# A selective-scan stage on one core: an earlier copy of dt * x to PSUM, B and C fetched apart, and empty pieces ahead of statistics

## The chip, the cores and the metric

The kernel runs as one program on one core of a Trainium2 chip. The metric is the device time of one execution in microseconds. The time before is the median of 3 runs.

## What is computed

The reference passes eight images of 56 x 56 positions and 128 channels through four layers. Layers 0, 2 and 3 are deformable convolutions with a small network behind them. Layer 1, which the change touches, is a "SS2D" block: a layer norm, a projection to 256 channels and a gate, a depthwise 3 x 3 convolution, a selective scan in four directions over all 3,136 positions, and an output part.

```python
x_dbl = jnp.einsum('bkdl,kcd->bkcl', xs, x_proj_w)
dts, Bsm, Csm = jnp.split(x_dbl, [R, R + N], axis=2)
dt = jax.nn.softplus(einsum('bkrl,kdr->bkdl', dts, dt_projs_w) + dt_projs_b)
A = -jnp.exp(A_logs).reshape(K, Di, N)
def step(h, t):
    dt_t, u_t, B_t, C_t = t
    h = h * jnp.exp(dt_t[..., None] * A) + (dt_t * u_t)[..., None] * B_t[:, :, None, :]
    y = jnp.einsum('bkdn,bkn->bkd', h, C_t)
    return (h, y)
...
y = _ln(y, out_norm_w, out_norm_b) * silu(z)
x = x + einsum('bhwd,cd->bhwc', y, out_proj_w)
x = x + fc2(gelu(fc1(_ln(x, norm2_w, norm2_b))))
```

There are Di = 256 channels with N = 16 states each, and K = 4 directions.

## The kernel before

**Tiling of the scan.** The positions of an image are cut into 4 chunks of SC = 784. A step is one image, one direction and one chunk: 8 x 4 x 4 = 128 steps, the directions in the order 1, 3, 0, 2. A step has 32 units. A unit holds 32 channels x 4 states on the 128 partitions and 784 positions along the free dimension. Units are numbered t = 4 cg + sg: cg is one of 8 groups of channels, sg one of 4 groups of states. "Group" below means the four units of one cg, "unit 4n" the first unit of group n.

**A unit.** `decay` (L1299) makes dA = exp(dt * A) on ACT into PSUM (two buffers). `inputs` (L1305, L1309) makes u = dt * x * B: for sg 0, 1 and 2 on VectorE (L1309), reading dt * x from PSUM, and for sg 3 on GpSimd (L1305, tile `up`), reading it from SBUF. The scan itself is one VectorE instruction (L1400, tile h, three buffers); its last column is kept for the next chunk by ACT (L1403). GpSimd multiplies with C (L1405, tile hc, six buffers). PE adds the 4 states of a channel (`add_sums`, L1331) into the PSUM tile `acc`, which `open_sums` (L1323) starts and `close_sums` (L1342, ACT) copies out every eight units.

**The copy.** `spread` (L1293) brings dt * x of one group into the PSUM tile `dtu`, which has one buffer, by two multiplications with the identity on PE. The new copy has to wait for the u of unit sg = 2 of the group before, the last that VectorE makes from that tile. It is asked for at the start of the iteration with sg = 2, two units ahead of its use.

**Fetches.** B and C of a step lie in DRAM in the tensor `rows`. `fetch_rows` (L1238) brings both for four states in one DMA, each row repeated over 32 partitions, into the tile bc (128 x 2 x 784, 784 KB, NSG + 1 = 5 buffers). The four fetches for the next step are asked for at t = 25, 29, 30, 31. `fetch_dt` (L1245) brings dt and dt * x of a group, two groups ahead, three buffers. All DMAs are issued from SP's queue.

**Work beside the scan.** `prepare` makes dt, B and C of the next step; it is a generator that is resumed at every even t. `input_stage` (the next image's norm, projection and convolution) and `output_stage` (norm, gate, projection, the two-layer network; 8 calls per image) are generators cut into pieces by `yield`; `advance(1)` runs one piece. It is called at odd t and where t % 8 == 4, which makes 20 places in a step, and at every t in the direction 2 of the last image. A piece is a few matmuls into the single-buffered PSUM tile `misc` and what reads them: `output_stage` transposes y on PE (L1130), takes statistics on VectorE (L1026, L1027), and later adds the projection to x on VectorE (L1153). Pieces left over at the end run after the last scan.

**What sets the order.** The program is traced in the order of the Python code, and a scheduler then sets the order of each engine's queue, which the engine keeps; `issue_after` (in `add_sums`) keeps the sums behind the last copy traced. The program order is therefore a wish and not the order of the queue.

Of the kernel before, what the change touches and what calls it, by code (L numbers as in the profile page):

```python
# [41 lines left out]
F32 = mybir.dt.float32  # L42
# [73 lines left out]
SC, SR = 784, 14  # L116
# [13 lines left out]
TC, TS = 32, 4  # L130
NCG, NSG = DI // TC, NST // TS
# [815 lines left out]
class Vss:  # L947
# [168 lines left out]
    def output_stage(self, i, c):  # L1116
        nc, w, n, T, m = self.nc, self.w, SH // self.NT, self.NT, SH
        y = self.bg.tile([128, NCH, m], F32, name="yin", tag="yin")
        nc.sync.dma_start(out=y, in_=self.sums[i][:, :, m * c : m * (c + 1)])
        sg = self.bg.tile([128, NCH, m], F32, name="sg", tag="sg")  # L1120
        nc.sync.dma_start(out=sg, in_=self.gates[i][:, NCH:, m * c : m * (c + 1)])
        yield
        yield
        z = self.bg.tile([128, T, DI], F32, name="z", tag="z")
        for t0 in range(0, T, 2):
            ps = self.misc()
            for t in range(2):
                at = n * (t0 + t)
                for ch in range(NCH):
                    nc.tensor.transpose(ps[:n, DI * t + 128 * ch : DI * t + 128 * (ch + 1)], y[:, ch, at : at + n], self.net.ident)  # L1130
            yield
            srcs = [ps[:n, DI * t : DI * (t + 1)] for t in range(2)]
            rs = self.stats(srcs)
            yield
            self.normalize(z[:, t0 : t0 + 2], srcs, rs)
            yield
        xt = self.bg.tile([128, T, C], F32, name="xt", tag="xt", bufs=2)
        nc.sync.dma_start(out=xt[:n], in_=self.rows_of(self.src[i], c, n))
        gT = self.bg.tile([128, NCH, m], F32, name="gT", tag="gT")
        for ch in range(NCH):  # L1140
            ps = self.misc()
            self.transpose(ps, [z[:n, t, 128 * ch : 128 * (ch + 1)] for t in range(T)])
            nc.scalar.activation(gT[:, ch, :], ps[:, :m], AF.Identity, bias=w["now_b"][:, ch : ch + 1], scale=w["now_w"][:, ch : ch + 1])
            yield
        nc.gpsimd.tensor_mul(gT, gT, sg)
        yield
        yield
        po = self.misc()
        for t in range(T):
            for ch in range(NCH):  # L1150
                nc.tensor.matmul(po[:n, 128 * t : 128 * (t + 1)], lhsT=gT[:, ch, n * t : n * (t + 1)], rhs=w["out"][:, ch, :], start=ch == 0, stop=ch == NCH - 1)
        yield
        nc.vector.tensor_add(xt[:n], xt[:n], po[:n].rearrange("p (t c) -> p t c", c=128))  # L1153
        srcs = [xt[:n, t, :] for t in range(T)]
        rs = self.stats(srcs)
        yield
        z = self.bg.tile([128, T, C], F32, name="z", tag="z", padded_shape=[128, T, DI])
        self.normalize(z, srcs, rs)
        yield
        ps = self.misc()  # L1160
        self.transpose(ps, [z[:n, t, :] for t in range(T)])
        xT = self.bg.tile([128, m], F32, name="xT", tag="xT")
        nc.scalar.activation(xT, ps[:, :m], AF.Identity, bias=w["n2b"], scale=w["n2w"])
        yield
        pre = self.bg.tile([128, NF, m], F32, name="pre", tag="pre", padded_shape=[128, NF, LC])
        for f in range(NF):
            ps = self.misc()
            nc.tensor.matmul(ps[:, :m], lhsT=w["fc1"][:, 128 * f : 128 * (f + 1)], rhs=xT, start=True, stop=True)
            nc.scalar.activation(pre[:, f, :], ps[:, :m], AF.Identity, bias=w["fc1_b"][:, f : f + 1])
            yield  # L1170
        last = nc.scalar.activation(pre, pre, AF.Gelu_apprx_tanh)
        with self.tc.issue_after(last.ins):
            nc.scalar.preload_act_table_set(EXP_LN)
        yield
        po = self.misc()
        self.net.bias_row(po, n, w["fc2_b"], T)
        for t in range(T):
            for f in range(NF):
                nc.tensor.matmul(po[:n, 128 * t : 128 * (t + 1)], lhsT=pre[:, f, n * t : n * (t + 1)], rhs=w["fc2"][:, f, :], start=False, stop=t == T - 1 and f == NF - 1)
            if t % 2:  # L1180
                yield
        nc.vector.tensor_add(xt[:n], xt[:n], po[:n].rearrange("p (t c) -> p t c", c=128))
        yield
        nc.sync.dma_start(out=self.rows_of(self.dst[i], c, n), in_=xt[:n])
        yield
# [44 lines left out]
            nc.sync.dma_start(out=s["dd"][128 * h : 128 * (h + 1)], in_=dd.rearrange("p x e -> p (x e)"))  # L1230
            yield

    def fetch_rows(self, s, sg):

        t = s["bc", sg] = self.work.tile([128, 2, SC], F32, name="bc", tag="bc", bufs=NSG + 1)
        r = s["rows"]
        src = bass.AP(tensor=r.tensor, offset=r.offset + TS * sg * 2 * SC, ap=[[0, TC], [2 * SC, TS], [1, 2 * SC]])
        self.nc.sync.dma_start(out=t.rearrange("p x e -> p (x e)"), in_=src)  # L1238

    def fetch_dt(self, s, cg):  # L1240

# [12 lines left out]
    def scans(self):  # L1254
        nc, w = self.nc, self.w
# [6 lines left out]
        units = [(at, t) for at in range(len(steps)) for t in range(NT)]  # L1262
# [5 lines left out]
            pass  # L1268
        for x in range(2):
            self.fetch_dt(state[0], x)  # L1270
        for x in range(NSG):
            self.fetch_rows(state[0], x)
        tasks = deque()

        def advance(count):
# [8 lines left out]
        def on_pool(t):  # L1284

            return order[t][1] == NSG - 1

        def spread(at, t):

            s, (cg, sg) = state[at], order[t]  # L1290
            ps = s["dtu", cg] = self.pdtu.tile([128, 2, 512], F32, name="dtu", tag="dtu")
            for b in range(2):
                last = nc.tensor.matmul(ps[:, b, :SH], lhsT=self.net.ident, rhs=s["dt", cg][:, 1, SH * b : SH * (b + 1)], start=True, stop=True)  # L1293
            self.last_spread = last.ins

        def decay(at, t):
            (i, k, c), s, (cg, sg) = steps[at], state[at], order[t]
            da = s["dA", t] = self.pda.tile([128, 1024], F32, name="dA", tag="dA")
            nc.scalar.activation(da[:, :SC], s["dt", cg][:, 0], AF.Exp, scale=w["A"][:, k, NSG * cg + sg : NSG * cg + sg + 1])  # L1299

        def inputs(at, t):
            s, (cg, sg) = state[at], order[t]
            if on_pool(t):
                u = self.work.tile([128, SC], F32, name="up", tag="up", bufs=1)
                nc.gpsimd.tensor_mul(u, s["dt", cg][:, 1], s["bc", sg][:, 0])  # L1305
            else:
                u = self.work.tile([128, SC], F32, name="u", tag="u", bufs=2)
                halves = [v.rearrange("p (x e) -> p x e", x=2) for v in (u, s["bc", sg][:, 0])]
                nc.vector.tensor_mul(halves[0], s["dtu", cg][:, :, :SH], halves[1])  # L1309
            s["u", t] = u  # L1310

# [43 lines left out]
        st = ready = None  # L1355
        group, late = [], deque()
        zeros = self.zeros()
        for x, (at, t) in enumerate(units):
            (i, k, c), s, (cg, sg) = steps[at], state[at], order[t]
            forward = k < 2  # L1360
            if t == 0:
# [8 lines left out]
                        self.load_xb(i + 1)  # L1370
                    ready = self.prepare(state[at + 1], *steps[at + 1][1:])
            if t % (2 * NSG) == 0:
                late.append((x + 5, open_sums, (at, t)))
            if sg == NSG - 2 and x + 2 < len(units):
                spread(*units[x + 2])
            while late and late[0][0] <= x:
                _, do, args = late.popleft()
                do(*args)
            if t % 2 == 0:
# [5 lines left out]
                    self.fetch_dt(state[to[0]], to[1])  # L1385
            if t in (3, 19):
                next(zeros, None)
            for g, when in enumerate((25, 29, 30, 31)):
                if t == when and at + 1 < len(steps):
                    self.fetch_rows(state[at + 1], g)  # L1390
            if x + 1 < len(units):
                decay(*units[x + 1])
                if not on_pool(units[x + 1][1]):
                    inputs(*units[x + 1])
            if x + 2 < len(units) and on_pool(units[x + 2][1]):
                inputs(*units[x + 2])
            hh = self.work.tile([128, SC], F32, name="h", tag="h", bufs=3)
            step = 1 if forward else -1
            u, dA = s.pop(("u", t)), s.pop(("dA", t))
# [2 lines left out]
                last = SC - 1 if forward else 0  # L1402
                nc.scalar.copy(st[:, t : t + 1], hh[:, last : last + 1])  # L1403
            hc = self.work.tile([128, SC], F32, name="hc", tag="hc", bufs=6)
            nc.gpsimd.tensor_mul(hc, hh, s["bc", sg][:, 1])  # L1405
            group.append((order[t], hc))
            if t % 2:
                late.append((x + 3, add_sums, (at, group)))
                group = []
                if t % (2 * NSG) == 2 * NSG - 1:  # L1410
                    late.append((x + 5, close_sums, (at, t)))
            if t % 2 or t % 8 == 4 or (i == self.images - 1 and k == 2):
                advance(1)
        for _ in zeros:
            pass
# [79 lines left out]
```

## Time and profile before

| | us |
|---|---|
| median of 3 runs (18,864.26 to 18,886.17) | 18,885.19 |
| the profiled execution, its own time | 18,880.74 |
| its span, first to last instruction | 18,879.1 |
| mean granted clock of PE | 0.802 |
| first unit of the scan to the last product | 2,450 to 14,006 |
| scan, L1400, from u (3,072) and from up (1,024), mean | 1.838 and 1.836 |
| u, L1309 (3,072), mean | 0.957 |
| hc, L1405 (4,096), mean | 1.871 |
| up, L1305 (1,024), mean | 1.854 |
| dA, L1299 (4,096), mean | 0.914 |

The profile is of one execution. Its first part gives each engine's busy time over the whole span, which holds three other layers. A row of windows gives, for a stretch of time, its length, the busy time and the count of records of PE, the weight load, DVE (VectorE), ACT (ScalarE) and POOL (GpSimd), then the granted clock of PE, the share of DMA and GB/s. A row of waits names who waited, for whom, and then us in total, times, and the longest. A row of the timeline has start, length, engine, line, operation, tiles and count, and in brackets the idle time ahead of it with what ended it. An fp32 matmul leaves two records.

### The profile page before, as it was taken

How to read it: one execution, taken by the hardware profiler on the slowest of the kernel's cores; microseconds unless marked ns; L12 is line 12 of the kernel's file. 1: busy time of each engine (PE TensorE's matmuls, PEld its weight loads, DVE VectorE, ACT ScalarE, POOL GpSimd, SP SyncE). 2: the span in 40 equal slices, each digit the busy share in tenths (PEclk: the TensorE clock that was granted, in tenths of full speed). 3: DMA queues.
4: the chain of work that ended last, by engine and by line, in shares of the span. 5: the costliest groups of instructions: out<-in, count | busy, mean ns of one | idle time of the engine just before them, and what ended most of it. 6: DMA issues, size and time to landing. Idle time of an engine off the chain costs nothing. (4 is left out here: it accounts for less than half of the span.)

```text
span 18879.1 us, 237115 instructions
## 1 busy us (share of the span) xinstructions
PE 14376.3 (76%) x79747; PEld 6872.9 (36%) x79747; DVE 15314.2 (81%) x18794; ACT 11192.3 (59%) x21363; POOL 11749.8 (62%) x6462
## 2 busy tenths in 40 slices
PE   6888777678778778778778778777666888577777
PEld 4555422222222222222222222222224666455555
DVE  7777379988988988988888889888967777677776
ACT  4665555566656666566566656656554666455555
POOL 1121079989988989989989989988961122111111
PEclk6777788889888888888888888888876777676666
DMA  8887544444433433444343443343326888588777
GB/s 240 227 222 217 133 156 158 164 156 155 146 138 142 142 141 142 143 144 142 140 143 138 145 143 140 141 146 131 141 99 172 216 214 211 155 205 211 206 211 178
DMA packets 1250535, 3112.19 MB, mean 165 GB/s; under 512 B 76608, under 2 KB 868180, under 8 KB 1181468
## 3 DMA queue, kind: packets, MB, share of 16 engines
q1 hardware_dynamic: 1249292, 3096.75, 53.5%
q8 instruction: 641, 10.50, 0.2%
q14 instruction: 602, 4.93, 0.1%
HBM read 2400.54 MB, written 872.17 MB: 173 GB/s over the span
## 5 line engine op out<-in xcount | busy, mean ns | idle before, releaser
L1405 POOL TENSOR_TENSOR hc<-h,bc 128x784 f32<-128x784 f32 x4096 | 7565.3, 1871 | 1008.9 <-DVE h L1400 774.5
L1400 DVE TENSOR_TENSOR_SCAN h<-dA,st,u 128x784 f32<-128x784 f32 x3072 | 5578.6, 1838 | 384.2 <-ACT dA L1299 267.4
L1299 ACT ACTIVATE dA<-dt,v_A 128x784 f32<-128x784 f32 x4096 | 3741.0, 914 | 787.1 <-DVE h L1400 783.5
L1331 PE MATMUL acc<-hc,v_sum 128*32 128x392 f32 x16384 | 3391.2, 563 | 89.2 <-POOL hc L1405 88.9
L1309 DVE TENSOR_TENSOR u<-dtu,bc 128x784 f32<-128x784 f32 x3072 | 2885.5, 957 | 586.7 <-PE dtu L1293 461.0
L1293 PE MATMUL dtu<-dt,ident 128*128 128x392 f32 x4096 | 2097.8, 639 | 1341.3 <-issue 932.4
L769 PE MATMUL pt<-ident,sw 112*128 112x112 f32 (+8 forms) x11648 | 1907.1, 302 | 476.5 <-DMA sw<-skew 470.4
L736 POOL MEMSET win<- 128x1820 f32 (+2 forms) x384 | 631.6, 1648 | 2487.8 <-DMA skew<-win 1950.0
L1400 DVE TENSOR_TENSOR_SCAN h<-dA,st,up 128x784 f32<-128x784 f32 x1024 | 1879.6, 1836 | 262.2 <-POOL hc L1405 132.9
L771 ACT COPY st<-pt 128x448 f32<-128x448 f32 (+6 forms) x2912 | 1228.7, 443 | 1326.3 <-PE pt L769 1282.6
L1403 ACT COPY st<-h 128x1 f32<-128x1 f32 x3072 | 580.1, 189 | 2276.1 <-DVE h L1400 2267.2
L1305 POOL TENSOR_TENSOR up<-dt,bc 128x784 f32<-128x784 f32 x1024 | 1898.5, 1854 | 36.5 <-DVE h L1400 30.9
L733 POOL TENSOR_TENSOR ay<-hat,om 112x756 f32<-112x756 f32 (+2 forms) x192 | 442.6, 2305 | 2154.2 <-ACT hat L729 1882.0
L1331 PEld LDWEIGHTS acc<-hc,v_sum 128*32 128x32 f32 x16384 | 800.8, 119 | 2600.5 <-issue 1711.8
L1293 PEld LDWEIGHTS dtu<-dt,ident 128*128 128x128 f32 x4096 | 855.0, 232 | 2403.2 <-issue 1474.4
L769 PEld LDWEIGHTS pt<-ident,sw 112*128 112x128 f32 (+8 forms) x11648 | 1336.6, 171 | 1056.7 <-issue 691.9
L745 DVE TENSOR_TENSOR win<-win,patch 112x252 f32 (+2 forms) x3456 | 1561.0, 461 | 52.9 <-DVE bn_st L847 14.4
L742 DVE TENSOR_TENSOR patch<-ay,hat 112x756 f32<-112x756 f32 (+2 forms) x1152 | 1221.7, 1074 | 446.7 <-POOL ay L733 446.4
L780 PE MATMUL yps<-st,xw 120*32 120x48 f32 (+8 forms) x23296 | 1221.0, 295 | 234.6 <-ACT st L771 190.6
L1069 PE MATMUL misc<-xn,v_tap 128*128 128x448 f32 x2016 | 882.3, 583 | 117.6 <-ACT xn L1103 63.3
L822 PE MATMUL ps<-xT,w_fc 128*128 128x448 f32 (+1 forms) x1536 | 800.1, 655 | 112.5 <-ACT xT L817 72.2
L1342 ACT COPY y<-acc 64x392 f32<-64x392 f32 x768 | 576.2, 750 | 450.3 <-PE acc L1331 440.5
(163 smaller groups left out, 19374.7 us busy)
## 6 DMA issues: line engine op xcount, KB each, us to landing
dt<-dds SPq DMA_DIRECT2D x1024, 784.0 KB
bc<-rows SPq DMA_DIRECT2D x512, 784.0 KB
sw<-skew SPq DMA_DIRECT2D x224, 1050.0 KB
sw<-skew SPq DMA_DIRECT2D x224, 896.0 KB
dds<-dd SPq DMA_DIRECT2D x256, 784.0 KB
sw<-skew SPq DMA_DIRECT2D x224, 784.0 KB
skew<-win SPq DMA_DIRECT2D x128, 964.7 KB
skew<-win SPq DMA_DIRECT2D x128, 771.8 KB
```

Of the source, the lines that this page charges most:

```text
L742: nc.vector.tensor_mul(patch[:n], bcast(a, 3, KX), bcast(b, 2, KY))
L745: self.last_add = nc.vector.tensor_add(to, to, patch[:n, NCB * p : NCB * (p + 1)]).ins
L769: last = nc.tensor.transpose(ps[:KP, n * g : n * (g + 1)], sw[t0:t1, g, KP * j : KP * (j + 1)], self.net.ident[t0:t1, t0:t1])
L771: nc.scalar.copy(st[:KP, : G * n], ps[:KP, : G * n])
L780: self.nc.tensor.matmul(yps[CG * g : CG * (g + 1), t0:t1], lhsT=xw[:KP, j, CG * g : CG * (g + 1)], rhs=st[:KP, n * g : n * (g + 1)], start ...
L1293: last = nc.tensor.matmul(ps[:, b, :SH], lhsT=self.net.ident, rhs=s["dt", cg][:, 1, SH * b : SH * (b + 1)], start=True, stop=True)
L1299: nc.scalar.activation(da[:, :SC], s["dt", cg][:, 0], AF.Exp, scale=w["A"][:, k, NSG * cg + sg : NSG * cg + sg + 1])
L1305: nc.gpsimd.tensor_mul(u, s["dt", cg][:, 1], s["bc", sg][:, 0])
L1309: nc.vector.tensor_mul(halves[0], s["dtu", cg][:, :, :SH], halves[1])
L1331: nc.tensor.matmul(acc[r : r + TC, :SH], lhsT=w["sum"], rhs=hc[:, SH * b : SH * (b + 1)], start=False, stop=sg == NSG - 1)
L1400: nc.vector.tensor_tensor_scan(hh[:, ::step], dA[:, :SC][:, ::step], u[:, ::step], st[:, t : t + 1], ALU.mult, ALU.add)
L1405: nc.gpsimd.tensor_mul(hc, hh, s["bc", sg][:, 1])
```

## The change

`spread` is asked for one iteration earlier (sg = NSG - 3), for three units ahead, directly after the `inputs` of the last u that reads the old copy. B and C get a tile, a fetch and five buffers each; B is asked for at t = 25, 28, 29, 30, C at t = 26, 29, 30, 31. `output_stage` gets an empty piece between the transposes of y and their statistics (twice per call) and one between the output projection and the addition that reads it. `advance` is called at t % 4 == 0 where it was t % 8 == 4, so 24 times in a step. The loop's variable x is renamed now.

```diff
@@ output_stage
                     nc.tensor.transpose(ps[:n, DI * t + 128 * ch : DI * t + 128 * (ch + 1)], y[:, ch, at : at + n], self.net.ident)
             yield
+            yield
             srcs = [ps[:n, DI * t : DI * (t + 1)] for t in range(2)]
             rs = self.stats(srcs)
...
         yield
+        yield
         nc.vector.tensor_add(xt[:n], xt[:n], po[:n].rearrange("p (t c) -> p t c", c=128))
@@ fetches
-    def fetch_rows(self, s, sg):
-
-        t = s["bc", sg] = self.work.tile([128, 2, SC], F32, name="bc", tag="bc", bufs=NSG + 1)
+    def fetch_row(self, s, x, sg):
+
+        name = "bc"[x]
+        t = s[name, sg] = self.work.tile([128, SC], F32, name=name, tag=name, bufs=NSG + 1)
         r = s["rows"]
-        src = bass.AP(tensor=r.tensor, offset=r.offset + TS * sg * 2 * SC, ap=[[0, TC], [2 * SC, TS], [1, 2 * SC]])
-        self.nc.sync.dma_start(out=t.rearrange("p x e -> p (x e)"), in_=src)
+        src = bass.AP(tensor=r.tensor, offset=r.offset + TS * sg * 2 * SC + x * SC, ap=[[0, TC], [2 * SC, TS], [1, SC]])
+        self.nc.sync.dma_start(out=t, in_=src)
@@ scans
-        for x in range(NSG):
-            self.fetch_rows(state[0], x)
+        for g in range(NSG):
+            for x in range(2):
+                self.fetch_row(state[0], x, g)
...
-            if sg == NSG - 2 and x + 2 < len(units):
-                spread(*units[x + 2])
-            while late and late[0][0] <= x:
+            while late and late[0][0] <= now:
...
-            for g, when in enumerate((25, 29, 30, 31)):
-                if t == when and at + 1 < len(steps):
-                    self.fetch_rows(state[at + 1], g)
-            if x + 1 < len(units):
-                decay(*units[x + 1])
-                if not on_pool(units[x + 1][1]):
-                    inputs(*units[x + 1])
+            for x, when in enumerate(((25, 28, 29, 30), (26, 29, 30, 31))):
+                if t in when and at + 1 < len(steps):
+                    self.fetch_row(state[at + 1], x, when.index(t))
+            if now + 1 < len(units):
+                decay(*units[now + 1])
+                if not on_pool(units[now + 1][1]):
+                    inputs(*units[now + 1])
+                if sg == NSG - 3 and now + 3 < len(units):
+                    spread(*units[now + 3])
...
-            if t % 2 or t % 8 == 4 or (i == self.images - 1 and k == 2):
+            if t % 2 or t % 4 == 0 or (i == self.images - 1 and k == 2):
                 advance(1)
```

The readers of bc change accordingly: `inputs` reads b, the product hc reads c.

More of the change, by code (lines that the diff above doesn't have):

```diff
@@ L1304, in inputs @@
                 u = self.work.tile([128, SC], F32, name="up", tag="up", bufs=1)
-                nc.gpsimd.tensor_mul(u, s["dt", cg][:, 1], s["bc", sg][:, 0])
+                nc.gpsimd.tensor_mul(u, s["dt", cg][:, 1], s["b", sg])
             else:
                 u = self.work.tile([128, SC], F32, name="u", tag="u", bufs=2)
-                halves = [v.rearrange("p (x e) -> p x e", x=2) for v in (u, s["bc", sg][:, 0])]
+                halves = [v.rearrange("p (x e) -> p x e", x=2) for v in (u, s["b", sg])]
                 nc.vector.tensor_mul(halves[0], s["dtu", cg][:, :, :SH], halves[1])
@@ L1357, in scans @@
         zeros = self.zeros()
-        for x, (at, t) in enumerate(units):
+        for now, (at, t) in enumerate(units):
             (i, k, c), s, (cg, sg) = steps[at], state[at], order[t]
@@ L1372, in scans @@
             if t % (2 * NSG) == 0:
-                late.append((x + 5, open_sums, (at, t)))
-            if sg == NSG - 2 and x + 2 < len(units):
-                spread(*units[x + 2])
-            while late and late[0][0] <= x:
+                late.append((now + 5, open_sums, (at, t)))
+            while late and late[0][0] <= now:
                 _, do, args = late.popleft()
@@ L1387, in scans @@
                 next(zeros, None)
-            for g, when in enumerate((25, 29, 30, 31)):
-                if t == when and at + 1 < len(steps):
-                    self.fetch_rows(state[at + 1], g)
-            if x + 1 < len(units):
-                decay(*units[x + 1])
-                if not on_pool(units[x + 1][1]):
-                    inputs(*units[x + 1])
-            if x + 2 < len(units) and on_pool(units[x + 2][1]):
-                inputs(*units[x + 2])
+            for x, when in enumerate(((25, 28, 29, 30), (26, 29, 30, 31))):
[7 more added lines that the diff above has]
+                    spread(*units[now + 3])
+            if now + 2 < len(units) and on_pool(units[now + 2][1]):
+                inputs(*units[now + 2])
             hh = self.work.tile([128, SC], F32, name="h", tag="h", bufs=3)
@@ L1404, in scans @@
             hc = self.work.tile([128, SC], F32, name="hc", tag="hc", bufs=6)
-            nc.gpsimd.tensor_mul(hc, hh, s["bc", sg][:, 1])
+            nc.gpsimd.tensor_mul(hc, hh, s["c", sg])
             group.append((order[t], hc))
             if t % 2:
-                late.append((x + 3, add_sums, (at, group)))
+                late.append((now + 3, add_sums, (at, group)))
                 group = []
                 if t % (2 * NSG) == 2 * NSG - 1:
-                    late.append((x + 5, close_sums, (at, t)))
-            if t % 2 or t % 8 == 4 or (i == self.images - 1 and k == 2):
+                    late.append((now + 5, close_sums, (at, t)))
+            if t % 2 or t % 4 == 0 or (i == self.images - 1 and k == 2):
                 advance(1)
```

## The prediction

> **What bounds the kernel now.** I read the page's first part, the windows by stage, the waits of VectorE in the scan stage, the fetch line with who waited for it, and one step boundary in the timeline.
>
> ```profile
> span 18879.1 us, 237115 instructions
> ...
> PE 14376.3 (76%) x79747; PEld 6872.9 (36%) x79747; DVE 15314.2 (81%) x18794; ACT 11192.3 (59%) x21363; POOL 11749.8 (62%) x6462
> ```
> No engine is near full over the whole span. The windows by stage (busy us of PE, weight load, DVE, ACT, POOL) split it:
> ```profile
> 2450.00:14006.00 11556.00, 8799.14 (x31339) 3000.00 (x31338) 10308.53 (x8615) 7066.77 (x13057) 10466.06 (x5766) 0.86 0.41 144
> 13310.00:13567.00 257.00, 171.34 (x604) 52.15 (x604) 235.85 (x169) 144.98 (x281) 253.09 (x141) 0.81 0.41 147
> 13567.00:13727.00 160.00, 85.98 (x352) 27.36 (x352) 155.61 (x113) 69.49 (x112) 145.59 (x81) 0.80 0.35 124
> ```
> The first row is the scan stage, the only one that the change touches: 11,556 us, POOL busy 90.6%, DVE 89.2%, PE 76%. Its 128 steps take 90.3 us each. The other rows are steps of the last image in which no background piece runs: 257/3 = 85.7 us with POOL 98.5% busy, and 160/2 = 80 us with DVE 97% busy where the next step's preparation is absent too. So two engines share the floor, about 5% below the mean step, and what lies between is waiting. What VectorE waited for in that stage:
> ```profile
> DVE u L1309 <- PE dtu L1293: 461.0, 266, 80.6
> DVE h L1400 <- ACT dA L1299: 297.2, 238, 3.9
> DVE h L1400 <- POOL hc L1405: 157.9, 183, 1.8
> DVE u L1309 <- DMA bc<-rows: 116.9, 95, 2.7
> DVE h L1400 <- POOL up L1305: 80.3, 80, 2.7
> DVE bn_st L1026 <- PE misc L1130: 53.1, 38, 3.3
> DVE xt L1153 <- PE misc L1151: 34.2, 17, 4.6
> ```
> 80.6 us of the first is the wait before the first unit; 380 us stay.
>
> **Part 1, B and C apart.** By unit of the step, 116.0 of the 116.9 us fall on unit 1 (94 of 128 steps), and 77.9 of the 80.3 us of `up` on unit 3 (78 steps). One boundary in the timeline shows why:
> ```profile
> 6029.79 7.39 POOL L1405 TENSOR_TENSOR hc<-h,bc 128x784 f32<-128x784 f32 x4
> 6031.69 4.22 SPq L1238 DMA_DIRECT2D bc<-rows  x3
> ...
> 6036.21 0.97 DVE L1309 TENSOR_TENSOR u<-dtu,bc 128x784 f32<-128x784 f32 x1 [1.47 <-DMA bc<-rows]
> ```
> The second fetch of a step goes into the buffer that hc of unit 28 reads: that product ends at 6029.79 + 1.87 = 6031.66, the fetch is issued 0.03 us later, and u of unit 1 starts 4.5 us after that. After the change B's buffer is freed by u of unit 28, which ended by 6025, some 6.7 us earlier: more than the waits (mean 1.2 us, longest 2.7). In the built order all four B fetches of most steps stand ahead of the C fetches that wait for hc, so SP's queue does not give this back, and `up`, queued behind only two or three products in 128 groups before, is so in 15 after. Gain: 116.0 + 77.9 = 194 us. C is freed as before and read by hc, later than u. Price: 512 DMAs more, 0.51 us of SP each, 263 us on a queue that nearly only waits; the dt fetches behind C waited behind the joint fetch before. Cover: that dt lands two groups ahead; were it gone, 0.5 us per fetch once per step, under 65 us. I take 0.
>
> The Trainium skill speaks against this part: "DMA: Bandwidth & Descriptors", section "Anatomy of one DMA", gives a fixed ~2.0 us per DMA plus bytes/436e9, stated there for the GpSimd path. An estimate from it: 803 KB takes 2.0 + 1.8 = 3.8 us, half takes 2.9, so two cost 2.0 us more, 512 x 2.0 = 1,024 us if all were waited for. The row has 4.5 us for the whole, and one fetch per step is waited for; halving it lands B 0.9 us sooner still. I go by the row.
>
> **Part 2, the copy.** It moves half an iteration ahead: behind u of unit 4n-2, ahead of the background piece of that iteration. The scheduler orders the queues itself, so I counted the built orders. Groups (of 1,024) with nothing between the last sum product and the copy: 419 before, 486 after. Groups whose u is queued two scans early (mean wait 1.69 us): 56 before, 35 after. PE now waits at the copy for that u with the piece and the next sums behind it; ACT's evictions and the six hc buffers wait for these. PE is idle 24% of the stage, so I take 0; at most the piece is late by one u, 0.95 us.
>
> **Part 3, more pieces per step.** `t % 8 == 4` becomes `t % 4 == 0`: 24 pieces a step for 20. An image has 105 input and 8 x 25 output pieces = 305 for 16 x 20 = 320 places; after, 8 x 28 + 105 = 329 for 384. The same work thus runs in 86% of the steps instead of 95%, so it is denser. A convolution piece is six matmul records, 882.3/2016 x 6 = 2.6 us of PE; a group has 2.05 us of copy (2097.8/1024) and 3.3 us of sums (3391.2/1024) besides, and DVE needs about 10.2 us for it (four scans of 1.84, three u of 0.957). Summing such rows along the built PE order: groups with over 12 us of PE work are 35 before, 83 after. In the trace the 35 cost 98 us of waiting for the copy, 2.8 each. Sorting all groups by PE work and by where u is queued, and giving the order of after the mean wait of each class, the 375 us of before become 477: **loss 102 us**. Bounds: -190 (the copy's place halves the wait, density harmless) and +335 (below).
>
> **Part 4, empty pieces.** They aim at 53.1 + 34.2 = 87 us. In the built order statistics queued at least three scans late grow only from 62 to 74%; bounds 0 and 87, I take 40. Empty pieces also displace work in the last image, where 32 places a step are too few: 92 places hold 92/25 = 3.7 stages before, 92/28 = 3.3 after. The timeline after the last scan has a stage every 43.3 us with nothing beside it, so 0.4 x 43 = **15 us are added** at the end. Close copies on ACT with only 5 or 6 units of lead fall from 788 to 620 of 1,024: about 20 of the 297 us.
>
> **Sum.** Waits: -194 - 40 - 20 + 102 = -152. Not all of it shows: POOL has 9.4% left on average and next to nothing in some steps, so "hc" becomes late next. I take 65%: -99. With the end: -99 + 15 = -84. The profiled execution took 18,880.7 (span 18,879.1), 4.5 below the median of the runs shown: 18,880.7 - 84 + 4.5 = 18,801, forecast 18,800.
>
> **Rivals.** (a) The copy's new place works in full: -194 - 190 - 87, 65% of it is -306, +15: 18,594, say 18,600. For it: 461 us is the largest wait. Against: the built order hardly changed there. Chance 0.12. (b) POOL takes it all back. The skill ("Perfetto Trace Analysis", "Identifying the Most-Contended Engine") says to optimize the engine with the highest occupancy; that is POOL, 90.6 against 89.2%, and nothing leaves POOL here, so its sum is 0 + 15: 18,900. The rows speak for it in three steps (98.5%), against it at the boundary, where POOL itself waited 1.83 us for the scan. Chance 0.15. (c) Slower: PE in the dense groups. If not 48 but all 66 added groups over 10 us (146 against 80) cost 2.8, that is +185 instead of +102, and ACT, whose queue holds dA behind evictions and close copies that wait for PE, grows by half, +150: 335 - 194 - 40 = +101, +15, about 19,000. It decides from where a heavy group costs about 5 us (239/48) instead of 2.8. For it: step 1 of each image already takes 95 to 101 us with dA late. Against: the last image runs 32 pieces a step at 86 to 98 us, no cliff. Chance 0.28. My forecast has 0.45, with its own range 18,720 to 18,860.
>
> **Chances and range.** A measurement tells 0.2% (38 us) from no change. Faster: 0.42 of the forecast's 0.45, and (a): 0.54. Same: 0.03 and most of (b): 0.17. Slower: (c) and the rest of (b): 0.29. Range 18,620 to 19,000: below it half of (a), above it half of (c), 0.2 together.
>
> **What would show it.** Right: the wait of u for B under 20 us in all, `up` at unit 3 gone, the copy wait near 480 us, 1 to 2 us less per step start, five stages with 15 us more after the last scan. Wrong: the copy wait under 300 (a); "h waits for hc" up by over 100 us with POOL at 92% (b); dA and copy waits together over 900 us and input steps over 95 us (c).

## The result, and the profile after

The changed kernel takes 18,766.6 us (median of 5 runs, 18,758.1 to 18,786.9) against 18,885.2 for the kernel before (5 runs, 18,864.3 to 18,903.6): a ratio of 0.9940, 95% interval 0.9928 to 0.9951. That is 118.6 us less; 85 less were forecast, and 18,767 lies inside the forecast's own range of 18,720 to 18,860. The profiled executions differ by 112.0 us of span, at the same granted clock (0.804, before 0.802).

The page of the changed kernel:

```profile
span 18767.1 us, 237758 instructions
...
PE 14211.3 (76%) x79747; PEld 6897.5 (37%) x79747; DVE 15283.9 (81%) x18794; ACT 11183.2 (60%) x21344; POOL 11721.8 (62%) x6462
```

No engine's work changed by more than 1.2%. Summed from the records, the time up to the first scan is 7.5 us longer, the scan stage (first scan to last) falls from 11,550.3 to 11,426.2, the output stages after the last scan grow from 201.2 to 215.3, and the other layers, which nobody touched, come out 9.7 us shorter: 7.5 - 124.1 + 14.1 - 9.7 = -112.2. So the stage is the place. Its windows, then the three steps and the two steps of the last image that were shown of before:

```profile
2440.00:13900.00 11460.00, 8649.31 (x31338) 3032.34 (x31339) 10266.37 (x8606) 7062.35 (x13051) 10445.43 (x5770) 0.86 0.42 146
...
13222.00:13471.00 249.00, 159.86 (x588) 49.01 (x588) 233.97 (x169) 139.04 (x269) 247.38 (x138) 0.84 0.41 145
13471.00:13629.00 158.00, 84.20 (x352) 27.18 (x352) 155.87 (x114) 69.40 (x112) 146.12 (x81) 0.82 0.35 128
```

POOL does the same work in less time (10,445 us of 11,460, 91.1%; before 90.6%). In the last row, steps with nothing beside the scan, a step takes 79 us instead of 80, with the same work on every engine. What went is waiting. VectorE's waits in the stage name it:

```profile
DVE u L1313 <- PE dtu L1297: 554.5, 251, 80.6
DVE h L1406 <- ACT dA L1303: 235.7, 196, 4.2
DVE h L1406 <- POOL hc L1411: 209.8, 164, 3.3
DVE xt L1184 <- PE misc L1181: 66.9, 25, 23.7
DVE xt L1155 <- PE misc L1152: 63.3, 24, 12.2
DVE bn_st L1026 <- PE misc L1130: 50.7, 37, 3.5
DVE bn_st L1026 <- DMA xt<-x: 35.8, 8, 6.2
...
DVE h L1406 <- POOL up L1309: 4.7, 5, 2.1
```

There is no row of u waiting for a fetch any more (116.9 us before), and `up` fell from 80.3 to 4.7. In exchange the wait for the copy rose from 461.0 to 554.5, of which 80.6 is again the first unit of all. This answer's window reaches some way past the last scan, so the xt and bn_st rows hold a little of the tail; within the stage they sum to 124 us, where before they had 91. And at the boundary between steps 39 and 40, where B of the second fetch had waited for a product of POOL:

```profile
6019.56 0.95 DVE L1313 TENSOR_TENSOR u<-dtu,b 128x784 f32<-128x784 f32 x1
6019.57 1.81 SPq L1241 DMA_DIRECT2D b<-rows  x3
...
6021.48 2.24 SPq L1241 DMA_DIRECT2D c<-rows  x2
...
6029.14 1.86 DVE L1313 TENSOR_TENSOR u<-dtu,b 128x784 f32<-128x784 f32 x2 [3.04 <-PE dtu L1297]
6029.93 0.51 SPq L1241 DMA_DIRECT2D c<-rows  x1
```

Three B fetches leave together, 11 us ahead of the step's first scan at 6030.92, and what still waits for POOL's product, the last C at 6029.93, is read only by hc. But the same fence shows the other side: u of this boundary waits 3.04 us for the copy on PE.

### The profile page after: what moved, and what is told of

Read it like the earlier page. It is cut to its first block, busy times and chain, and to the rows that moved or that the text cites. A ratio compares the mean times of both kernels' runs of the same rounds, so it can differ in the third digit from the quotient of the medians.

```text
span 18767.1 us, 237758 instructions
## 1 busy us (share of the span) xinstructions
PE 14211.3 (76%) x79747; PEld 6897.5 (37%) x79747; DVE 15283.9 (81%) x18794; ACT 11183.2 (60%) x21344; POOL 11721.8 (62%) x6462
## 5 line engine op out<-in xcount | busy, mean ns | idle before, releaser
L1411 POOL TENSOR_TENSOR hc<-h,c 128x784 f32<-128x784 f32 x4096 | 7539.9, 1870 | 772.6 <-DVE h L1406 541.5
L1313 DVE TENSOR_TENSOR u<-dtu,b 128x784 f32<-128x784 f32 x3072 | 2871.5, 956 | 559.1 <-PE dtu L1297 554.5
L1335 PE MATMUL acc<-hc,v_sum 128*32 128x392 f32 x16384 | 3212.8, 551 | 102.8 <-POOL hc L1411 102.1
L1309 POOL TENSOR_TENSOR up<-dt,b 128x784 f32<-128x784 f32 x1024 | 1904.6, 1860 | 135.1 <-DVE h L1406 124.0
```

The costliest lines, as they stand in the source:

```text
L1309: nc.gpsimd.tensor_mul(u, s["dt", cg][:, 1], s["b", sg])
L1335: nc.tensor.matmul(acc[r : r + TC, :SH], lhsT=w["sum"], rhs=hc[:, SH * b : SH * (b + 1)], start=False, stop=sg == NSG - 1)
L1411: nc.gpsimd.tensor_mul(hc, hh, s["c", sg])
```

## The experiments

**The theories.** Mine, from the prediction and these rows: the fetch of B gives about 194 us of waits, more places per step cost about 100 through PE, the copy's place gives nothing, and POOL takes part of the gain back. The rivals: the copy's place matters (a); POOL's work is the floor, so that the fetch gain alone would vanish (b); and, within the fetch, that it is the smaller transfer and not the earlier release of the buffer that helps. Four kernels take one part each, four combine parts, one puts B behind C again, and three vary where the places are. The twelve were timed in three groups, each beside the kernel before on the same chip; its medians were 18,870.0, 18,873.6 and 18,884.3 (18,885.2 beside the whole change). The differences below are taken from each kernel's own before, because these medians alone are up to 15 us apart.

| kernel | median us | ratio to before, 95% |
|---|---|---|
| B and C apart | 18,621.8 | 0.9864, 0.9849 to 0.9879 |
| copy asked earlier | 18,883.8 | 1.0005, 0.9996 to 1.0014 |
| 24 places | 18,855.9 | 0.9989, 0.9980 to 0.9998 |
| empty pieces | 18,793.8 | 0.9955, 0.9941 to 0.9968 |
| apart + copy + empties (20 places) | 18,635.3 | 0.9873, 0.9857 to 0.9888 |
| apart + 24 places | 18,689.4 | 0.9902, 0.9887 to 0.9917 |
| apart + empties | 18,634.8 | 0.9871, 0.9855 to 0.9886 |
| apart + empties + 24 places | 18,736.1 | 0.9925, 0.9912 to 0.9939 |
| *whole change* | 18,766.6 | 0.9940, 0.9928 to 0.9951 |
| apart, B held behind C | 18,885.5 | 1.0004, 0.9995 to 1.0013 |
| apart, 24 places for output pieces only | 18,714.0 | 0.9913, 0.9898 to 0.9928 |
| apart, 24 places for input pieces only | 18,759.1 | 0.9936, 0.9922 to 0.9949 |
| apart, 24 for output, 16 for input pieces | 18,531.8 | 0.9816, 0.9803 to 0.9830 |

### B and C apart, alone

The kernel before with the fetch part of the diff and nothing else.

```diff
-            for g, when in enumerate((25, 29, 30, 31)):
-                if t == when and at + 1 < len(steps):
-                    self.fetch_rows(state[at + 1], g)
+            for e, when in enumerate(((25, 28, 29, 30), (26, 29, 30, 31))):
+                if t in when and at + 1 < len(steps):
+                    self.fetch_row(state[at + 1], e, when.index(t))
```

> Only B and C are fetched apart; copy, pieces and places stay as before. Theory (the late B is the gain): the 117 us of u waiting for the fetch and the 78 us of the first up of a step vanish; with 65 to 100% of it realized and nothing given back elsewhere, 125 to 195 us faster: 18,690 to 18,760, below the full change. Rival (the copy's place is the gain, GpSimd takes back what B sets free): within 40 us of before, 18,850 to 18,925, with the wait of the scan for hc up by 100 us or more.

Measured: 248 us less, beyond the 125 to 195 expected and more than twice what the whole change gives. Its stage, and VectorE's waits in it:

```profile
2441.00:13751.00 11310.00, 8726.88 (x31328) 2974.21 (x31326) 10281.81 (x8614) 7068.00 (x13066) 10456.87 (x5764) 0.87 0.42 148
```
```profile
DVE u L1310 <- PE dtu L1294: 453.9, 251, 82.9
DVE h L1401 <- ACT dA L1300: 306.9, 213, 4.5
DVE h L1401 <- POOL hc L1406: 162.6, 175, 2.9
...
DVE h L1401 <- POOL up L1306: 8.5, 7, 2.2
```

The two waits lost 116.9 and 71.8 us, 188.7 together. The copy, dA and hc stand as they stood before (380, 297 and 158 without the first unit; here 371, 307 and 163). VectorE's idle time in the stage falls by 216.6 us and the stage by 240.6. The other 24 us come from overlap: where one VectorE instruction follows another without a wait, their records overlap by about 0.1 us (two scans in a row take 3.58 us, one 1.84). Over the stage the records overlap by 559.7 us before and by 592.7 here, while their sum is 9 us larger. Nothing became late next, with POOL at 92.5%. Rival (b) falls: it said that this part is worth nothing.

### B behind C: release or size?

As the kernel just shown, with the same tiles and the same 1,024 transfers of half the size, but each B fetch held behind the C fetch of its group in SP's queue.

```diff
+            for g, when in enumerate((25, 29, 30, 31)):
+                if t == when and at + 1 < len(steps):
+                    c_row = self.fetch_row(state[at + 1], 1, g)
+                    with self.tc.issue_after(c_row.ins):
+                        self.fetch_row(state[at + 1], 0, g)
```

> B and C are fetched apart, but each B fetch is held in SP's queue behind the C fetch of the same states, so that B leaves when the product hc of unit 28 ends, as the joint fetch did; all else as before. Theory (the early release of B's buffer is the gain, not the smaller transfer): the waits of u for B and of the scan for up come back, together 100 to 190 us, and the time is 18,780 to 18,870. Rival (two small transfers are the gain): 18,600 to 18,680.

```profile
DVE u L1310 <- PE dtu L1294: 379.9, 252, 7.2
DVE h L1403 <- ACT dA L1300: 290.9, 224, 4.8
DVE h L1403 <- POOL hc L1408: 168.4, 194, 1.8
DVE u L1310 <- DMA b<-rows: 136.4, 101, 3.0
DVE h L1403 <- POOL up L1306: 86.2, 82, 3.8
```

Measured: the time before (1.0004, just above the range expected), and both waits are back (136.4 and 86.2, before 116.9 and 80.3; the window leaves the first unit out). So two small transfers are not a gain in themselves.

This run alone does not separate release from size, because here B also moves behind C. At the boundary between steps 39 and 40, C was issued at 6037.24, B at 6037.80, and u of unit 1 started at 6042.28:

```profile
6037.24 0.51 SPq L1238 DMA_DIRECT2D c<-rows  x1
6037.80 0.60 SPq L1238 DMA_DIRECT2D b<-rows  x1
...
6042.28 0.97 DVE L1310 TENSOR_TENSOR u<-dtu,b 128x784 f32<-128x784 f32 x1 [2.00 <-DMA b<-rows]
```

By the packets, B's data began to move at 6039.94, when most of C's had gone. The traces of the other kernels settle it. Where nothing else was issued in the 6.5 us ahead, the last packet of a joint fetch ended 3.96 us after its issue (median of 110, before), that of a B fetch 2.80 us (median of 34, apart alone). So half the size does land sooner, by about 1.2 us. But from the issue of the second B to u of unit 1 there are 4.62 us before (median of 127 steps) and 9.95 with B and C apart, never less than 5.15. The longest of the 110 joint fetches took 5.03, so by these times a fetch of the whole size would have come in time too. It is the release: B leaves when u has read the old B, and no longer waits until hc has read C.

### The copy asked earlier, alone

```diff
-            if sg == NSG - 2 and x + 2 < len(units):
-                spread(*units[x + 2])
...
+                if sg == NSG - 3 and x + 3 < len(units):
+                    spread(*units[x + 3])
```

> Only the copy of dt * x is asked for half an iteration earlier. Theory: the queue order of PE hardly moves, the wait for the copy stays near 380 us (379 by the classes of the trace of before), time within 40 us of before: 18,850 to 18,925. Rival (the copy is the gain): the wait for the copy falls by 100 us or more, 18,800 or less.

Measured: no difference that this measurement tells (+14 us, interval -8 to +26). The copy wait is 403.6 us where it was 380.4, so it did not fall. Rival (a) falls.

### 24 places, alone and on top

The condition of `advance` is the only edit, on the kernel before, on the one with B and C apart, and in reverse on the whole change.

```diff
-            if t % 2 or t % 8 == 4 or (i == self.images - 1 and k == 2):
+            if t % 2 or t % 4 == 0 or (i == self.images - 1 and k == 2):
                 advance(1)
```

> Only the 24 places for pieces in a step in place of 20. Theory (denser pieces cost PE): the wait for the copy rises from 380 to about 455 us, and 50 to 100 us slower: 18,935 to 18,985. Rival (density is free because the last steps of an image are emptied by it): within 40 us of before or faster, with steps 11 and 12 near 79 us.

> The fetches apart plus 24 places in a step, nothing else. Theory (density): the wait for the copy rises from 371 us with the fetches alone to about 450, and the time from 18,622 to 18,700 to 18,760. Rival (density costs nothing with any fetch, as it cost nothing alone): 18,590 to 18,650.

> The full change with 20 places for pieces in a step, as before, in place of 24. Theory (the denser pieces eat what the fetches give): the wait for the copy falls from 474 to about 365 us and the time to that of the fetches alone, 18,580 to 18,660. Rival (the three other parts collide among themselves, density is innocent): as the full change, 18,730 to 18,800.

Measured: on the kernel before, 14 us less, where 50 to 100 more were expected: the theory failed there. With B and C apart, 64 more, a little under the expected cost. In the whole change, 120 more. The copy wait grows each time: 380 to 435, 371 to 440, 442 to 474. With the late joint fetch the 55 us are made up for by others: the waits of the statistics, dA, bc and st fall by 48, 43, 40 and 13, while those of the additions and of `up` rise by 23 and 25. A reading that fits, and that no run isolates: part of what a dense group makes late was late there anyway, and with B early that cover is gone. This is the part that eats the gain: the whole change at 20 places is 18,635, as fast as B and C apart alone within the intervals. The expectation for it had the time right and the wait wrong: about 365 us for the copy, measured 442.

### Empty pieces, alone and on top

```diff
             yield
+            yield
             srcs = [ps[:n, DI * t : DI * (t + 1)] for t in range(2)]
...
         yield
+        yield
         nc.vector.tensor_add(xt[:n], xt[:n], po[:n].rearrange("p (t c) -> p t c", c=128))
```

> Only the three empty pieces per output call; 20 places in a step. Theory: of the 87 us that statistics and the addition wait for PE, less than half goes, the end after the last scan is 15 us longer: within 40 us of before, 18,850 to 18,925. Rival (the empty pieces are the gain): those waits fall under 20 us and the time under 18,830.

> The fetches apart plus the empty pieces, 20 places in a step, copy as before. If gains add: 18,622 - 76 = 18,546. Theory: the empty pieces alone gained mostly where the late fetch was in play (that wait fell by 41 us of its 117 there), so less is left for them: 18,560 to 18,630. Rival (empty pieces and early B collide): over 18,680.

Measured: 76 us less alone, where less than 40 was expected, and 9 more with B and C apart, which the intervals do not tell from nothing. Alone, the waits for bc, dA and hc fall by 42, 44 and 29; the statistics' own wait falls only from 53.1 to 42.6 and that of the additions rises from 38 to 53. So they do not work by what they were put ahead of. The 329 pieces of an image do not fit in its 320 places, so that the images come out uneven (1,417 to 1,467 us each from the second to the last; before 1,440 to 1,458), and the pieces meet the scan at other points. Why this kernel gains 76 us is not settled. The tail is 214 to 216 us in every kernel with empty pieces, and 196 to 202 in all without.

### The whole change without the copy's move

> The full change with the copy of dt * x where it was. Theory (the copy's place does nothing): as the full change, 18,730 to 18,800, wait for the copy 475 to 510 us. Rival (the early copy blocks PE's queue and is what the full change loses by): 18,560 to 18,660.

Measured: 18,736.1, 19 us less than the whole change against each one's own before (31 by the medians); the ratios' intervals overlap a little. VectorE's waits show the trade:

```profile
DVE u L1312 <- PE dtu L1296: 540.9, 279, 8.6
DVE h L1403 <- ACT dA L1302: 214.2, 199, 3.8
DVE h L1403 <- POOL hc L1408: 165.3, 150, 4.6
```

The move does cut the copy's own wait here, from 540.9 to 473.9, but dA and hc are 21 and 45 us more with it. At 20 places it is worth nothing (18,635.3 with, 18,634.8 without), and the copy's wait is longer with it, 442 against 404.

### Which pieces are too dense

Three kernels with B and C apart and nothing else but a number of places that depends on what stands at the head of the queue of pieces.

```diff
-            if t % 2 or t % 8 == 4 or (...):
+            if t % 2 or t % 8 == 4 or (t % 8 == 0 and tasks and tasks[0].__name__ == "output_stage") or (...):
```

> The fetches apart; 24 places in a step while an output call is at the head of the background work, 20 while the input stage is. If density costs through the convolution pieces alone: as the fetches alone, 18,600 to 18,650. If output pieces carry it too: 18,660 to 18,710.

> The fetches apart; 24 places in a step while the input stage is at the head, 20 while an output call is. If density costs through the convolution pieces: 18,660 to 18,710. If not: 18,600 to 18,650.

Measured: 24 places for output pieces alone cost 78 us over B and C apart, for input pieces alone 123, both beyond what was expected. Both at once had cost 64. So the two do not add up, and which of them is to blame stays open: the copy wait is 475 and 474 us in the two, dA 154 and 295, hc 220 and 158. What can be said is that each alone costs.

The last one goes the other way with the input pieces, which hold the convolution:

```diff
-            if t % 2 or t % 8 == 4 or (...):
+            if t % 2 or (t % 4 == 0 and tasks and tasks[0].__name__ == "output_stage") or (...):
```

> The fetches apart; 24 places for output calls and 16 for the input stage, so that the heavy convolution pieces stand thinner. Theory: the wait for the copy falls under the 371 us of the fetches alone, to about 320, and the time to 18,570 to 18,620. Rival: the denser output pieces give back as much, 18,630 to 18,680.

Measured: 18,531.8 us, 1.84% under the kernel before (interval 1.70 to 1.97), the fastest of all and below the range expected. It differs from the kernel with 24 places for output pieces only in the 16 for input pieces, and is 182 us faster than that one. With 20 places for output pieces and 16 for input pieces nothing was run. One step, the seventh of the third image, in before, in the changed kernel and in this one:

```profile
5861.09:5950.72 89.63, 78.60 (x255) 26.33 (x252) 80.05 (x70) 60.14 (x117) 81.45 (x45) 0.92 0.40 140
```
```profile
5840.40:5938.12 97.72, 83.23 (x278) 26.54 (x276) 79.57 (x66) 63.90 (x116) 81.78 (x47) 0.95 0.40 137
```
```profile
5778.48:5864.50 86.02, 71.92 (x233) 23.40 (x230) 78.82 (x65) 57.23 (x107) 81.84 (x46) 0.88 0.41 146
```

VectorE and POOL do the same work, 79 to 80 and 81 to 82 us, in all three. PE has 278 matmul records in the changed kernel, 255 before, 233 here, and in these three the step's length goes with them. It is no rule. The same step with B and C apart and 24 places, and in the whole change at 20 places:

```profile
5816.97:5905.67 88.70, 78.12 (x254) 26.30 (x252) 78.63 (x57) 60.96 (x106) 81.96 (x47) 0.90 0.38 138
```
```profile
5754.08:5849.49 95.41, 76.71 (x247) 24.51 (x245) 82.61 (x89) 62.46 (x130) 82.60 (x47) 0.87 0.44 156
```

The second is among the long ones with fewer records than before. So a count per step does not tell the cost; where the pieces stand between two copies can. That is seen in the timeline of the step in the changed kernel:

```profile
5903.09 1.51 PE L1335 MATMUL acc<-hc,v_sum 128*32 128x392 f32 x8
...
5904.53 4.78 PE L1069 MATMUL misc<-xn,v_tap 128*128 128x448 f32 x12
...
5909.24 1.64 PE L1327 MATMUL acc<-y,ident 128*64 128x392 f32 x4
...
5913.87 0.93 PE L1297 MATMUL dtu<-dt,ident 128*128 128x392 f32 x2
...
5916.54 0.97 DVE L1313 TENSOR_TENSOR u<-dtu,b 128x784 f32<-128x784 f32 x1 [5.38 <-PE dtu L1297]
```

Two convolution pieces in a row (12 records, 4.78 us) and the sums stand ahead of the copy in PE's queue, and VectorE, with all its inputs but this one, waits 5.38 us. With the 16 places its waits in the stage are:

```profile
DVE u L1310 <- PE dtu L1294: 387.2, 209, 83.0
DVE h L1401 <- ACT dA L1300: 213.0, 189, 4.7
DVE h L1401 <- POOL hc L1406: 182.9, 191, 2.1
```

The copy waits 304.2 us without the first unit (371.0 at 20 places) and dA 94 us less than there; POOL's products 20 more.

## Why the prediction was right, and where it was not

**B and C apart** (forecast: 194 us of waits gone). Right in cause and size: the two rows fell by 192.5 us (116.9 and 75.6), u no longer waits for B at all, and the kernel with B held behind C, together with the 9.95 us from issue to use, shows that it is the release. The price of 512 more DMAs was taken as 0, with up to 65 us. The Trainium skill ("DMA: Bandwidth & Descriptors", section "Anatomy of one DMA") has a fixed cost of about 2.0 us per DMA, stated there for the GpSimd path. The prediction's estimates from it, 3.8 us for the whole and 2.9 for the half, are close to the 3.96 and 2.80 us that the traces show from the issue on SP's queue to the last packet. What the traces do not bear out is adding the cost up over all 512: B held behind C, with the same 512 more, took the time of before (1.0004).

**POOL is late next** (forecast: 65% of the sum is realized, so hc becomes late next). This step is wrong, though hc did rise, by 51.9 us, just about the 53 that the discount took off. With B and C apart alone, with POOL at 92.5%, hc rose by 5 us, and 189 us of waits gone took 241 us from the stage. hc rose in some kernels with dense pieces (221 with 24 places, 220 with 24 for output pieces) and not in others (158 with 24 for input pieces). A mean busy share of 90.6% was read as a floor. It is one in single steps only: the changed kernel's three steps with preparation have POOL at 99.3%, its two without at 92.5%, and the fetch gain lies at the boundaries, where POOL itself waited. Rival (b) leaned on the skill's "Perfetto Trace Analysis", section "Identifying the Most-Contended Engine", that one should optimize the engine with the highest occupancy. By that measure it was POOL, at 90.6%; no work left POOL, and 248 us went.

**The copy's place** (0). Right in sum: alone +14, not told from 0; at 20 places 0; at 24 perhaps 19 to 31 us lost. Its own wait rises by 23 us alone and by 38 at 20 places, and falls by 67 at 24, where dA and hc take it back: the bound of -190 was never near.

**More places** (+102, all of it in the copy wait). The wait went from 380.4 to 473.9, +93.5, for 375 to 477 forecast. The number was hit with luck: the places were to make all of it, but the whole change at 20 places already has 442.1, so the last four places add only 32 there. Without the copy's move they add 137 (404.0 to 540.9), on the kernel before 55, with B and C apart 69. What a place costs depends on the other parts, and the price of the edit in time is not the wait either: 120 us within the whole change, 64 with B and C apart, -14 on the kernel before. The count of PE work per group had no term for this. The copy waits expected of the single kernels show the same: near 450 with B and C apart and 24 places (measured 440), about 320 with the 16 places (304) and 455 with 24 places alone (435), but 365 for the whole change at 20 places (442) and 475 to 510 without the copy's move (541).

**Empty pieces** (-40 of 87 us of waits) failed. Within the stage of the whole change those waits grew from 91 to 124 us: the statistics fell by 13, but the two additions rose by 10 and, new, the statistics of the next image's x waited 35.8 us for their own fetch. The end of 15 us was right (14.1, five stages), although 0.4 x 43, as it is written, gives 17.

**Close copies** (-20): dA fell by 61.5. The direction was right, the size was too small.

**The sum.** Waits of -152 were forecast and 65% of that, -99, for the stage. The idle time of VectorE in the stage fell by 82.0 us (1,244.6 to 1,162.6), the stage by 124.1. The other 42 us are VectorE's busy time, in which overlapping records count once (10,305.6 to 10,263.6 us). Of these, 29 are more overlap, 559.7 to 588.4 us, and 13 a smaller sum of the records. The prediction had no term for the overlap. So the forecast lands where it should in good part by luck. After the discount it had -126 for the fetch and +42 for the rest, the end included. Measured are -248 for the fetch alone and +130 for what the rest does on top: both are far too small, and they cancel.

**The signs** named ahead: the u wait for B under 20 (0), `up` gone (4.7), the copy wait near 480 (473.9, of which 442 stood there without the added places), 1 to 2 us less per step start (79 for 80 us where nothing else runs), and five stages 15 us longer at the end. None of those that would have shown it wrong came up: dA and the copy wait together are 710 us and POOL is at 91%. Only the mean of some convolution steps reached what rival (c) said: in images 2 to 7 the seventh step is 100.3 us on average where it was 89.9, and the thirteenth, emptied of pieces, 78.7 where it was 85.6.

**What stays open**: why empty pieces alone give 76 us and nothing on top; why dense output pieces and dense input pieces cost 78 and 123 us one at a time and 64 together; which of its two numbers makes the fastest kernel fast; a joint fetch with one buffer more was not tried, nor the whole change without its empty pieces.

## What to carry to other kernels

A tile whose halves have different last readers is free only when the later one is done: where the half that is needed first is released first, give it a tile and a fetch of its own, and check in the queue that nothing later is ahead of it. Judge each part of a composite change by itself: here one part gave 248 us and the others together gave 130 back. And try the density of background pieces by kind: here 16 places for the convolution's pieces in place of 20, with 24 for the output pieces, took 182 us off, while 24 for the convolution's alone cost 123. Why is not shown: over the steps of images 2 to 7 the fastest kernel is not the most even one in PE records.

## What the runs showed of the hardware

A fetch of 784 KB that was issued with nothing close ahead of it had its last packet 3.96 us after its issue (median of 110), one of 392 KB 2.80 us (median of 34): half the size took seven tenths of the time. Behind another 392 KB on the same queue, issued 0.56 us earlier, it took 4.5 us at one boundary. With 73,732 more packets in the whole run (1,324,267 against 1,250,535), the kernel with B held behind C took the time of before. And 189 us of waits on VectorE, once gone, took 241 us from the stage while POOL was busy for over 90% of it: that share said nothing of which waits were in series with the end.
